# A transformer block in float32: where norm steps, value transfers and loads stand among the attention slots

## The chip, the cores and the metric

The kernel runs on one core of a Trainium2 chip, in float32. The metric is the device time of one execution in microseconds (us), lower is better. The times of the kernel before are the median of three runs.

## What is computed

One transformer block for x of 2 × 1024 × 256 with a context of 2 × 154 × 192 and 16 heads of 64. Cut to what matters:

```python
h = layernorm(x, ln1_g, ln1_b)
x = attention(h, h, sa_wq, sa_wk, sa_wv, sa_wo, sa_bo) + x      # 1024 keys
h = layernorm(x, ln2_g, ln2_b)
x = attention(h, ctx, ca_wq, ca_wk, ca_wv, ca_wo, ca_bo) + x    # 154 keys
h = layernorm(x, ln3_g, ln3_b)
a, gate = split(h @ ff_w1 + ff_b1)
return a * gelu(gate) @ ff_w2 + ff_b2 + x
```

`attention` projects q, k and v, takes a softmax of q k / 8 for every head, weighs v with it, and projects the heads together through `wo`. `layernorm` subtracts the mean of a row of 256, divides by its deviation, and applies a gain and a shift.

## The kernel before

The work runs in *units*: a unit is one batch and one pair of heads, 16 in all (units 0 to 7 are batch 0). The main loop goes through three stages, each in *slots*: 128 slots of self attention (`SA`, eight a unit, two *halves* of `SH` = 4), 48 of context attention (`CA`, three a unit), 64 of the feed-forward part (`FF`). Rows are counted in tiles of 128, eight tiles a batch.

A slot p of self attention does this. TensorE computes the scores of two groups of rows (`scores`, L442) into two PSUM tiles, of which the next slot's scores want the same memory. VectorE takes their maxima (L602), ScalarE the exponents (L453, four instructions), and four small DMAs on SP's queue (`exchange`, L463) carry maxima and sums between partitions. GpSimd and ScalarE join them (`join`, L471 to L479), VectorE takes a reciprocal `rd` (L549), GpSimd scales the weights (L553, four instructions), VectorE transposes them (L567). Two slots later (`LAG` = 2) `self_values` weighs the values with them (L489, `po`); it takes two slots of each four. In the other slots `run_work` gives TensorE a *piece*: for the next unit a query projection (`pq`, L327), a key projection (`pk`, also L327), the values (`pv`, L352), or a tile of the output projection (`py`, L420). These are queues in Python, and the order in which they are emptied is the order of instructions: `work` holds pieces, `outs` output tiles, `side` norm steps, `later` small leftovers (bias additions), `stores`, `adds` and `lates` the second halves of things begun earlier.

`run_work(n, n_side, bank)` takes pieces from `work` worth n banks, then up to `n_side` steps from `side`, whose needs must be met (the output tiles that they read must have been added to x), then output tiles. In self attention it is called in slots 0, 1, 4 and 5 of each unit (and in all of the first half of unit 0), with `n_side` 1.

A normalization is made beside other work, `norm_beside` building its steps. For context attention's batch 0 and for self attention a step concerns one tile, for context attention's batch 1 (not `narrow`) two. A step has up to four parts, for different tiles: `stats` on VectorE (L210, L211), `deviation` (L216, L220), `normalize` (L223: `off` on VectorE at L226, then `xn` on ScalarE at L235, one instruction a tile), and `turn`, four TensorE transposes into a bank (`ph`, L244) whose store (L254, L258) writes `hT`, the input of the projections.

Values of a unit are projected by `project_self_values`, either whole or in two half pieces (`parts` = 2 for the units 1 to 4, that is while `ui < HP`, with `HP` = 4). Its store copies the result on ScalarE (L361) and then sends each copy across to the other half of the partitions by transfers on SP's queue (L365, L366), per tile for a half piece, and for all tiles at once for a whole one.

`self_beside(ui)` runs at the start of each unit and fills the queues: pieces for the next unit, output tiles of a batch and half that are ready, the self norm of batch 1 at `ui == 1` and the context norm of batch 0 at `ui == NPAIR + HP` (12). `load_ahead` issues weight loads for the unit after next. At the seam, `self_drain` finishes the last slots of self attention inside the first slots of context attention. `cross_beside` fills the queues in context attention, loads its keys' and values' weights, and starts the context norm of batch 1.

At the very start x is loaded by both DMA queues, and the columns of the first norm's gain and shift by ACT's queue (L105 to L110).

Of the kernel before, what the change touches and what calls it, by code (L numbers as in the profile page):

```python
# [9 lines left out]
AF = mybir.ActivationFunctionType  # L10
# [8 lines left out]
def tile_transformer_block(ctx: ExitStack, tc: tile.TileContext, a: dict, out: bass.AP):  # L19
# [84 lines left out]
        load_x(nc.scalar, 0, NT // 2 + t)  # L104
    for n in names[:2]:  # L105
        for r0 in range(0, P, HR):
            nc.scalar.dma_start(
                out=cols[r0:r0 + HR, row_of[n]:row_of[n] + NH],
                in_=w[n].rearrange("(r p) -> p r", p=HR),
            )  # L110
# [80 lines left out]
    def norm_pieces(kind, b, first=False):  # L191

        ln = {"sa": "ln1", "ca": "ln2", "ff": "ln3"}[kind]
        g0, b0 = row_of[ln + "_g"], row_of[ln + "_b"]
        st = {}
        nh = NC if kind == "ff" else NH  # L200
        order = tile_order(kind)

        def stats(t):
            if t == 0:
                st["hT"] = hT[kind, b] = p2.tile(
                    [P, nh, NC * S // nh], F32, tag="hT", name=f"hT_{ln}_{b}")
            if t % 2 == 0:
                st["mv", t] = small.tile([P, 2, 2], F32, tag="mv", name=f"mv_{ln}_{b}_{t}")
            s6 = small.tile([P, 6], F32, tag="st", name=f"st_{ln}_{b}_{t}")
            nc.vector.bn_stats(s6, xt[b, order[t] // GT][:, order[t] % GT, :])  # L210
            nc.vector.bn_aggr(st["mv", t // 2 * 2][:, t % 2, :], s6)  # L211

        def deviation(t):
            mv = st["mv", t]
            var = small.tile([P, 2], F32, tag="var", name=f"var_{ln}_{b}_{t}")
            (nc.vector if first else nc.gpsimd).tensor_scalar(  # L216
                var, mv[:, :, 1], EPS, 1.0, op0=ALU.add, op1=ALU.mult
            )
            rstd = small.tile([P, 2], F32, tag="rstd", name=f"rstd_{ln}_{b}_{t}")
            nc.gpsimd.tensor_tensor(rstd, var, power, ALU.pow)  # L220
            st["rstd", t] = rstd

        def normalize(t):  # L223
            rstd = st["rstd", t]
            off = small.tile([P, 2], F32, tag="off", name=f"off_{ln}_{b}_{t}")
            nc.vector.scalar_tensor_tensor(  # L226
                off, st["mv", t][:, :, 0], -1.0, rstd, op0=ALU.mult, op1=ALU.mult
            )
            pool, tag = (one, "xn") if narrow(kind, b) and not first else (pp_, "P")

            xn = pool.tile([P, nh, 2, D // nh], F32, tag=tag, name=f"xn_{ln}_{b}_{t}")
            st["xn", t] = xn
            for i in range(2):
                xs = xt[b, order[t + i] // GT][:, order[t + i] % GT, :]
                nc.scalar.activation(  # L235
                    xn[:, :, i, :], xs.rearrange("p (c d) -> p c d", c=nh), AF.Identity,
                    bias=off[:, i:i + 1], scale=rstd[:, i:i + 1],
                )

        def turn(t):  # L240
            ph = spare["bank"](f"ph_{ln}_{b}_{t}").rearrange("p (c k) -> p c k", c=nh)
            for i in range(2 * D // P):

                nc.tensor.transpose(  # L244
                    ph.rearrange("p c k -> p (c k)")[:, i * P:(i + 1) * P],
                    st["xn", t].rearrange("p c i d -> p (c i d)")[:, i * P:(i + 1) * P], ident)

            def store():
                k = NC * 2 * P // nh
                for c in range(nh):  # L250
                    own = st["hT"][:, c, t // 2 * k:(t // 2 + 1) * k]
                    gain, shift = cols[:, g0 + c:g0 + c + 1], cols[:, b0 + c:b0 + c + 1]
                    if first and (c < nh // 2 or t % 4 == 0):
                        nc.vector.tensor_scalar(  # L254
                            own, ph[:, c, :], gain, shift, op0=ALU.mult, op1=ALU.add
                        )
                    else:
                        nc.scalar.activation(  # L258
                            own, ph[:, c, :], AF.Identity, bias=shift, scale=gain
                        )  # L260

            return store

        return (
            [lambda t=t: stats(t) for t in range(NT)],
            *([lambda t=t, f=f: f(t) for t in range(0, NT, 2)] for f in (deviation, normalize, turn)),
        )

# [6 lines left out]
    def narrow(kind, b):  # L275

        return kind == "sa" or kind == "ca" and b < B - 1
# [68 lines left out]
    def project_self_values(v, pv, wt, h, i0, n):  # L346

        for i in range(i0, i0 + n):
            for c in range(NH):
                for r in range(2):  # L350
                    own = slice(r * HR, (r + 1) * HR)
                    nc.tensor.matmul(  # L352
                        pv[r][:, i * P:(i + 1) * P], lhsT=h[own, c, i * P:(i + 1) * P],
                        rhs=wt[own, c, :], start=(c == 0), stop=(c == NH - 1),
                        tile_position=(r * HR, 0),
                    )

        def store():
            tiles = [slice(r * GT + i0, r * GT + i0 + n) for r in range(2)]
            for r in range(2):  # L360
                nc.scalar.copy(  # L361
                    v[:, tiles[r], 0, :],
                    pv[r][:, i0 * P:(i0 + n) * P].rearrange("p (t d) -> p t d", d=P))
            for own in [slice(0, NT)] if n == GT else tiles:
                nc.sync.dma_start(out=v[:QG, own, 1, :], in_=v[QG:, own, 0, :])  # L365
                nc.sync.dma_start(out=v[QG:, own, 1, :], in_=v[:QG, own, 0, :])  # L366

        return store

# [126 lines left out]

    work, outs = [], []
    side, lates = [], []
    stores, adds = [], []
    later = []  # L500

# [5 lines left out]
    def flush(queue):  # L507
        for fn in queue:
            fn()
        queue.clear()  # L510
# [22 lines left out]
    def out_pieces(kind, b, half, tiles):  # L533
        outs.extend(lambda t=t: out_piece(kind, b, half, t) for t in tiles)
# [79 lines left out]

    def self_beside(ui):

        parts = 2 if ui < HP else 1
        nxt = self_pieces(*units[ui + 1], parts) if ui + 1 < NU else cross_pieces(*units[0], KB)
        if ui + 1 < NU:
            work.extend(nxt)  # L620
        else:

            work.extend(nxt[:1])
            held.extend(nxt[1:])
        if ui >= HP:
            ob, oh = divmod((ui - HP) // HP, 2)
            t0 = (ui % HP) * 2
            out_pieces("sa", ob, oh, (t0, t0 + 1))
        if ui == 1:
            norm_beside("sa", 1)  # L630
        if ui in (HP, HP + 2):
            add_biases("sa", (ui - HP) // 2)
        if ui == NPAIR + HP:
            norm_beside("ca", 0)

    def load_ahead(p):

        ui, n = divmod(p, 2 * SH)
        for what in "qkv":
            at = {"q": 2, "k": 3, "v": 2 * SH - 1}[what] + 3 * (ui == 0 and what != "v")  # L640
            if n != at:
                continue
            if ui + 2 < NU:
                load_weights("sa", units[ui + 2][1], what)
            elif ui + 2 == NU or what == "q":
                load_weights("ca", units[ui + 2 - NU][1], what)

    def self_drain(p):

        late = scale_groups(*joins.pop(0)) if joins else None  # L650
        if p - LAG < SA:
            turn_groups(p - LAG)
        if late:
            late()


    CG = [(t, min(TG, NT - t)) for t in range(0, NT, TG)]
# [168 lines left out]
    def cross_beside(ui):  # L826

        if ui + 1 < NU:
            for what in "kv":
                load_weights("ca", units[ui + 1][1], what)  # L830
            pieces = cross_pieces(*units[ui + 1])
            work.extend(pieces[:2])
            held.extend(pieces[2:])
        if ui == 3:
            norm_beside("ca", B - 1)
        if ui > HP + 1:
            ob, oh = divmod((ui - HP - 2) // HP, 2)
            t0 = ((ui - HP - 2) % HP) * 2
            out_pieces("ca", ob, oh, (t0, t0 + 1))
        if ui == NPAIR + HP + 1:  # L840
            norm_beside("ff", 0)
# [97 lines left out]
    with tc.manual_schedule():  # L939
# [45 lines left out]
        for p in range(SA):  # L985
# [15 lines left out]
            load_ahead(p)  # L1001
            h, hg = divmod(p, SH)
            if h == 0 or hg < LAG:
                run_work(2 if p < SA - SH else 1, 1, sum_tile)
            else:
                run(lambda: self_values(h - 1, hg - LAG))

        for c in range(CA):
# [21 lines left out]
            flush(adds)  # L1030
            then = cross_first(c)
            flush(stores)
            flush(lates)
            lates.append(then())
            if c <= SH:
# [69 lines left out]
```

## Time and profile before

| What | us |
|---|---|
| median of three runs | 1174.38 (1170.46 to 1174.64) |
| the profiled execution: its own time | 1176.44 |
| the profiled execution: its span, from first to last instruction | 1174.6 |

The stages of that execution, by windows that begin at the first instruction of a slot:

| Stage | from to | length | PE busy |
|---|---|---|---|
| start, up to the first scores | 0.00 to 20.35 | 20.35 | 14.84 |
| self attention, slots 0 to 7 | 20.35 to 64.46 | 44.11 | 39.95 |
| slots 8 to 16 (first slot of unit 2) | 64.46 to 115.52 | 51.06 | 44.17 |
| units 12 to 14 | 553.94 to 690.72 | 136.78 | 134.84 |
| unit 15 | 690.72 to 732.90 | 42.18 | 39.78 |
| context attention, first five slots | 732.90 to 755.31 | 22.41 | 19.96 |
| context attention, the rest | 755.31 to 975.56 | 220.25 | 213.72 |
| feed-forward | 975.56 to 1174.60 | 199.04 | 195.49 |

The page names engines by short names: PE is TensorE's matrix multiplication, PEld its weight load, DVE VectorE, ACT ScalarE, POOL GpSimd, SP the engine that here only issues DMAs. A name with q, such as SPq, is an engine's queue of issues. "L442" is a line of the kernel. A number in brackets after a line is idle time of the engine before it, and the arrow says what ended it.

### The profile page before, as it was taken

What the parts mean: (1) busy time and instruction counts of PE and PEld (TensorE: products, weight loads), DVE (VectorE), ACT (ScalarE), POOL (GpSimd) and SP (SyncE); (2) the same over time, 40 slices, a digit from 0 to 9 for tenths busy, and PEclk for the clock granted to TensorE, in tenths of its full rate; (3) what the DMA queues carried; (4) which work ended last, traced back from release to release, by engine and by line L of the source; (5) the groups of instructions that cost most, each with busy time, mean ns of one, the idle gap of its engine ahead of it and who ended that gap; (6) DMA issues with size and microseconds to landing.
All of it is one profiled execution on the core that took longest, in us unless ns stands there. A gap on an engine that the chain in (4) does not pass through costs nothing.

```text
span 1174.6 us, 36750 instructions
## 1 busy us (share of the span) xinstructions
PE 1135.7 (97%) x14343; PEld 684.0 (58%) x14343; DVE 834.8 (71%) x1184; ACT 653.0 (56%) x2095; POOL 666.4 (57%) x1556
## 2 busy tenths in 40 slices
PE   8889999999999999999999999998999999999998
PEld 5444444455555545545545554564666667888887
DVE  4778988889898998989998899556565674232222
ACT  5656777666665665756666766547655573041111
POOL 1657777787887777777777777546454453030000
PEclk9989999999999999999999999999999999999999
DMA  2231111111111111101101010157544443000000
GB/s 77 74 92 30 39 30 30 37 33 39 30 35 39 30 31 39 39 21 39 46 14 39 25 28 16 46 138 183 139 116 112 112 93 73 1 18 10 18 9 18
DMA packets 105215, 59.94 MB, mean 51 GB/s; under 512 B 32394, under 2 KB 95826, under 8 KB 105042
## 3 DMA queue, kind: packets, MB, share of 16 engines
q1 hardware_dynamic: 101138, 54.84, 19.6%
q10 hardware_dynamic: 3904, 2.76, 0.8%
q8 instruction: 113, 1.85, 0.7%
q14 instruction: 60, 0.49, 0.1%
HBM read 27.91 MB, written 2.10 MB: 26 GB/s over the span
## 4 chain that ended last, share of the span: by engine, by line
PE 72%; ACT 9%; DMA 5%; POOL 4%; DVE 3%; SPq 3%; issue 3%; ACTq 0%; DVEq 0%; POOLq 0%
PE po L489 14%; PE s L442 12%; PE pa L894 9%; ACT p L453 6%; PE py_ca L420 5%; PE pq_ca L327 5%; PE pf L917 5%; PE py_sa L420 4%; DMA st<-st 4%; PE poc L807 4%; PE pv_sa L352 3%; PE sc L728 3%; PE pq_sa L327 3%; SPq L463 2%; PE pk_sa L327 2%
## 5 line engine op out<-in xcount | busy, mean ns | idle before, releaser
L453 ACT ACTIVATE p<-s,st 128x512 f32<-128x512 f32 x512 | 344.9, 687 | 201.8 <-DVE st L602 198.7
L553 POOL TENSOR_SCALAR p<-p,rd,ee 128x512 f32<-128x512 f32 x512 | 385.6, 767 | 44.7 <-DVE rd L549 43.7
L602 DVE TENSOR_REDUCE st<-s 128x2 f32<-128x1024 f32 x256 | 301.4, 1219 | 32.3 <-PE s L442 17.2
L567 DVE STREAM_TRANSPOSE pT<-p 128x1024 f32<-128x1024 f32 x256 | 302.4, 1219 | 1.5 <-POOL p L553 1.5
L442 PE MATMUL s<-k_sa,q_sa 64*32 64x512 f32 x4096 | 257.1, 597 | 19.3 <-ACT p L453 18.2
L489 PE MATMUL po<-pT,v_sa 64*64 64x256 f32 x4096 | 235.8, 379 | 0.0
L489 PEld LDWEIGHTS po<-pT,v_sa 64*64 64x64 f32 x4096 | 150.4, 133 | 109.1 <-issue 34.4
L755 POOL TENSOR_SCALAR p<-p,rden 128x154 f32<-128x154 f32 x256 | 96.8, 398 | 117.0 <-DVE rden L752 116.5
L442 PEld LDWEIGHTS s<-k_sa,q_sa 64*32 64x32 f32 x4096 | 63.8, 106 | 145.8 <-ACT p L453 68.7
L744 ACT ACTIVATE p<-sc,neg 128x154 f32<-128x154 f32 x256 | 95.7, 394 | 83.2 <-DVE rden L752 77.5
L894 PE MATMUL pa<-hT_ln,wf 128*128 128x256 f32 x512 | 121.0, 379 | 0.0
L903 DVE SCALAR_TENSOR_TENSOR u<-pa,cols,gate 128x256 f32<-128x256 f32 x64 | 31.0, 484 | 124.4 <-ACT gate L900 124.4
L900 ACT ACTIVATE gate<-pa,cols 128x256 f32<-128x256 f32 x64 | 30.3, 473 | 151.5 <-PE pa L894 151.5
L894 PEld LDWEIGHTS pa<-hT_ln,wf 128*128 128x128 f32 x512 | 96.8, 190 | 13.7 <-DVE u L903 0.4
L453 ACT ACTIVATION_READ_ACCUMULATOR p<-s,st 128x1 f32 x512 | 104.6, 204 | 0.0
L733 DVE TENSOR_REDUCE neg<-sc 128x6 f32<-128x924 f32 (+1 forms) x48 | 48.6, 1012 | 56.0 <-PE sc L728 55.9
L352 PEld LDWEIGHTS pv_sa<-sa_wv,hT_ln 64*128 64x128 f32 x1024 | 59.6, 188 | 19.9 <-issue 8.4
L327 PE MATMUL pq_ca<-hT_ln,ca_wq 64*128 64x512 f32 (+1 forms) x304 | 64.9, 616 | 5.1 <-ACT hT_ln L258 3.0
L477 POOL TENSOR_TENSOR zz<-ee,st 128x8 f32<-128x8 f32 x128 | 25.9, 202 | 73.6 <-ACT ee L475 73.6
L352 PE MATMUL pv_sa<-sa_wv,hT_ln 64*128 64x128 f32 x1024 | 64.0, 276 | 1.8 <-ACT k_sa L341 1.2
L917 PE MATMUL pf<-wf,u 128*128 128x256 f32 x256 | 65.0, 379 | 0.2 <-DVE u L903 0.2
L549 DVE RECIPROCAL rd<-den 128x4 f32<-128x4 f32 x128 | 22.6, 177 | 57.2 <-POOL den L479 51.7
(80 smaller groups left out, 1289.1 us busy)
## 6 DMA issues: line engine op xcount, KB each, us to landing
wf<-pT_ca SPq DMA_DIRECT2D x128, 128.0 KB, 2.5
st<-st SPq DMA_DIRECT2D x512, 1.0 KB, 1.8
v_sa<-v_sa SPq DMA_DIRECT2D x22, 256.0 KB, 3.5
sa_wq<-in_L_xattn_sa_wq_dram SPq DMA_DIRECT2D x32, 128.0 KB, 3.0
sa_wk<-in_L_xattn_sa_wk_dram SPq DMA_DIRECT2D x32, 128.0 KB, 3.3
sa_wv<-in_L_xattn_sa_wv_dram SPq DMA_DIRECT2D x32, 128.0 KB, 3.5
ca_wq<-in_L_xattn_ca_wq_dram SPq DMA_DIRECT2D x32, 128.0 KB, 2.9
wf<-in_L_xattn_ff_w_dram SPq DMA_DIRECT2D x12, 256.0 KB, 3.5
```

What stands on the lines that cost most here:

```text
L327: nc.tensor.matmul(pq[r][f:f + m, t0:t0 + n], lhsT=wt[own, c, f:f + m], rhs=h[own, c, t0:t0 + n], start=(c == 0), stop=(c == NH - 1), tile ...
L352: nc.tensor.matmul(pv[r][:, i * P:(i + 1) * P], lhsT=h[own, c, i * P:(i + 1) * P], rhs=wt[own, c, :], start=(c == 0), stop=(c == NH - 1), ...
L420: nc.tensor.matmul(py[:, :D], lhsT=o[:, i, t * P:(t + 1) * P], rhs=wo[kind][:, half * HP + i, :], start=(i == 0), stop=(i == HP - 1),)
L442: nc.tensor.matmul(sc[a4 * KB:(a4 + 1) * KB, j, :], lhsT=q[r, c:c + KB], rhs=k[r, h * HB:(h + 1) * HB], start=True, stop=True, tile_positi ...
L453: nc.scalar.activation(pr[:, j, :], sc[:, j, :], AF.Exp, bias=st[:, 0, 0, i, j:j + 1], accum_out=st[:, 0, 1, i, j:j + 1],)
L489: nc.tensor.matmul(po[a2][j * DH:(j + 1) * DH, :QH // 2], lhsT=v[r, t, e, j * DH:(j + 1) * DH], rhs=pT[r, j * NK + n, :], start=(t == 0 an ...
L553: nc.gpsimd.tensor_scalar(pr[:, j, :], pr[:, j, :], rd[:, c:c + 1], ee[:, 0, c:c + 1], op0=ALU.mult, op1=ALU.mult,)
L567: nc.vector.transpose(halves[h][:, :, c:c + KB], groups.pop(0).rearrange("p j (n k) -> p (j n) k", k=KB))
L602: nc.vector.tensor_reduce(st[:, 0, 0, i, :], sc[i], AX.X, ALU.max, negate=True)
L755: nc.gpsimd.tensor_scalar(pr_[:, j, i, :T], pr_[:, j, i, :T], rden[:, j, i:i + 1], 1.0, op0=ALU.mult, op1=ALU.mult,)
L894: nc.tensor.matmul(pa[:, half, :TF * P], lhsT=w1[:, c, half * DF + f * P:half * DF + (f + 1) * P], rhs=h[:, c, t0 * P:(t0 + TF) * P], star ...
L917: nc.tensor.matmul(sums[blk][i][:, :D], lhsT=sums[blk, "u"][:, f, i * P:(i + 1) * P], rhs=w2[:, f, :], start=(f == 0), stop=(f == NF - 1),)
```

## The change

- The columns of `ln1_b` are loaded by SP's queue instead of ACT's.
- The two transfers of values across partitions come once a unit, after the last copy, for all tiles.
- `parts` is 2 only for `0 < ui < HP`: unit 1's values, made in unit 0, come in one piece. The first unit then has six pieces.
- `run_work` is called with `n_side` of 1 only in slots 4 and 5 of a unit (`h` odd) and in the first half of unit 0; in slots 0 and 1 it takes no norm step.
- The context norm of batch 0 begins at unit 9 instead of unit 12. Output tiles are made in the order 0, 4, 1, 5, …, the one in which the norm reads them.
- In the context norm of batch 1, `xn` is made on GpSimd by a multiply and an add with per-row scalars, instead of on ScalarE.
- The key weights of context attention's unit 1 are loaded in slot 126, instead of in the first slot of context attention.
- At the seam, the reciprocal and the scaling of `self_drain` are put behind the first reduction of the next slot.

```diff
-            nc.scalar.dma_start(
+            (nc.scalar if n == names[0] else nc.sync).dma_start(
...
-                nc.scalar.activation(
-                    xn[:, :, i, :], xs.rearrange("p (c d) -> p c d", c=nh), AF.Identity,
-                    bias=off[:, i:i + 1], scale=rstd[:, i:i + 1],
-                )
+                xs, own = xs.rearrange("p (c d) -> p c d", c=nh), xn[:, :, i, :]
+                if kind == "ca" and not narrow(kind, b):
+                    nc.gpsimd.tensor_scalar(
+                        own, xs, rstd[:, i:i + 1], off[:, i:i + 1], op0=ALU.mult, op1=ALU.add)
+                else:
+                    nc.scalar.activation(
+                        own, xs, AF.Identity, bias=off[:, i:i + 1], scale=rstd[:, i:i + 1])
...
-            for own in [slice(0, NT)] if n == GT else tiles:
-                nc.sync.dma_start(out=v[:QG, own, 1, :], in_=v[QG:, own, 0, :])
-                nc.sync.dma_start(out=v[QG:, own, 1, :], in_=v[:QG, own, 0, :])
+            if i0 + n == GT:
+                nc.sync.dma_start(out=v[:QG, :, 1, :], in_=v[QG:, :, 0, :])
+                nc.sync.dma_start(out=v[QG:, :, 1, :], in_=v[:QG, :, 0, :])
...
+    drain = []
...
-        parts = 2 if ui < HP else 1
+        parts = 2 if 0 < ui < HP else 1
...
-            out_pieces("sa", ob, oh, (t0, t0 + 1))
+            out_pieces("sa", ob, oh, tile_order("ca")[t0:t0 + 2])
...
-        if ui == NPAIR + HP:
+        if ui == NPAIR + 1:
             norm_beside("ca", 0)
...
+        if p == SA - 2:
+            load_weights("ca", units[1][1], "k")
...
-        late = scale_groups(*joins.pop(0)) if joins else None
+        if joins:
+            drain.append(scale_groups(*joins.pop(0)))
         if p - LAG < SA:
             turn_groups(p - LAG)
-        if late:
-            late()
...
-            for what in "kv":
+            for what in "kv" if ui else "":
...
-                run_work(2 if p < SA - SH else 1, 1, sum_tile)
+
+                run_work(2 if p < SA - SH else 1, h % 2 or h == 0, sum_tile)
...
             flush(stores)
+            flush(drain)
             flush(lates)
```

## The prediction

> **What bounds the kernel now.** I read the page first, then busy time by stage, then the timeline and the waits of the stages in which TensorE is not full.
>
> From the page of the kernel before:
>
> ```profile
> span 1174.6 us, 36750 instructions
> ...
> PE 1135.7 (97%) x14343; PEld 684.0 (58%) x14343; DVE 834.8 (71%) x1184; ACT 653.0 (56%) x2095; POOL 666.4 (57%) x1556
> ...
> PE 72%; ACT 9%; DMA 5%; POOL 4%; DVE 3%; SPq 3%; issue 3%; ACTq 0%; DVEq 0%; POOLq 0%
> ```
>
> TensorE is the bound, and 38.9 us of the span are not covered by it. The chain that ended last still leaves TensorE for 28% of its length, so single places run on other engines. The windows (start and end; length, PE busy and matmuls; granted clock; DMA share; GB/s), cut at slot starts, tell where:
>
> ```profile
> 64.46:115.52 51.06, 44.17 (x709) 0.93 0.22 54
> 115.52:160.96 45.44, 42.70 (x716) 1.00 0.14 33
> ...
> 293.14:336.58 43.44, 43.44 (x724) 1.00 0.15 34
> ...
> 553.94:597.75 43.81, 43.68 (x725) 1.00 0.14 33
> 597.75:644.93 47.18, 45.85 (x733) 1.00 0.14 31
> 644.93:690.72 45.79, 45.31 (x733) 1.00 0.13 29
> ...
> 732.90:755.31 22.41, 19.96 (x164) 0.92 0.17 48
> ...
> 799.57:815.34 15.77, 13.47 (x109) 0.89 0.60 140
> 815.34:833.60 18.26, 15.53 (x117) 0.91 0.60 154
> ```
>
> A unit of self attention (eight slots) costs 43.44 us where nothing waits. The first full one, at 64.46, costs 51.06; units 13 and 14 (597.75 and 644.93) carry eight more matmuls, the norm's turns, and cost 3.4 and 2.0 us more than unit 12; then come the seam between the attentions (732.90) and the context attention around its norm (799.57 to 833.60). The clock is below 1.00 in just the windows with long waits. The feed-forward part, 199.04 us with 195.49 busy, is untouched.
>
> Why slots 7 to 9 are slow, from the timeline (start, length, engine, operation; in brackets the idle time and what ended it):
>
> ```profile
> 61.20 0.60 SPq L365 DMA_DIRECT2D v_sa<-v_sa  x1
> 61.85 0.60 SPq L366 DMA_DIRECT2D v_sa<-v_sa  x1
> 62.61 3.39 SPq L463 DMA_DIRECT2D st<-st  x4
> ...
> 67.31 0.20 POOL L471 TENSOR_TENSOR dd<-st 128x4 f32<-128x4 f32 x1 [3.48 <-DMA st<-st]
> ...
> 68.04 0.21 ACT L475 ACTIVATE ee<-dd 128x8 f32<-128x8 f32 x1 [3.15 <-POOL dd L473]
> ...
> 71.90 0.66 PE L442 MATMUL s<-k_sa,q_sa 64*32 64x512 f32 x8 [3.51 <-ACT p L453]
> ```
>
> Value transfers occupy SP's queue, the exchange of maxima (`st`) goes out behind them, GpSimd waits for it, then ScalarE, then the scores.
>
> And in context attention, two lines of its timeline:
>
> ```profile
> 801.20 1.09 ACT L235 ACTIVATE xn_ln<-x,off_ln,rstd_ln 128x256 f32<-128x256 f32 x2 [1.80 <-DVE off_ln L226]
> ...
> 803.37 1.20 PE L327 MATMUL pq_ca<-hT_ln,ca_wq 64*128 64x512 f32 x2 [1.89 <-ACT v_ca L701]
> ```
>
> ScalarE stands still before `xn`, and the copies of `v_ca` behind it hold a bank that TensorE's query projection wants. The waits of that stretch also name `hT_ln` (2.7 us), made on ScalarE after `xn`.
>
> **What the Trainium skill says.** "TensorE: Matmul & The Clock Gate", section "HAM oscillation — how this bites in real kernels": idle gaps of over about 3.4 us throttle TensorE. The trace agrees in kind: from 76 to 82 us it shows a clock of 0.68, from 804 to 809 of 0.72, from 820 to 825 of 0.66, each behind such waits. So a long wait costs its length plus (1 − 0.68) × 6.0 = 1.9, 1.4 and 1.7 us. "DMA: Bandwidth & Descriptors", "Issuing engines are not separate DMA queues": issuing elsewhere saves sequencer time only. Here an issue takes 0.60 us on SP, so fewer issues help although the bytes stay. "GPSIMD Engine Reference", 3.1: 512 elements of a one-input operation took 769 ns; the trace has 767 ns (L553). "SBUF — State Buffer", "SBUF: two separate sides": a GpSimd operation and some VectorE ones exclude each other; no wait in this trace shows it for `xn`, and it is my upper cost there.
>
> **Part by part.** The order of instructions of the two kernels shows equal numbers of matmuls and VectorE operations; SP issues about 27 transfers fewer. So everything comes from waits. Sums are against the profiled execution, 1176.44 us (span 1174.6), 2.06 above the median of 1174.38.
>
> 1. *Column loads of ln1_b go from ACT's to SP's queue.* ACT issued them from 4.74 to 6.01 and loaded its table at 6.04; the first `xn` ran at 7.34, its `off` ready at 6.74. Gain at most 7.34 − 6.74 = 0.6; on SP they delay sa_wq, so 0 is the other end. −0.4.
>
> 2. *Two value transfers a unit, six pieces in the first unit.* Four of 64 KB (4 × 0.62 = 2.5 us of SP) stood behind each half. Now two of 256 KB (1.06 + 0.64 us, as at 278.91) follow the second half: 3.3 us of SP less in each halved unit. Unit 1's values, which before had their second half in slot 8, come whole in slot 5, and all later pieces move one slot up. Slot 8 (64.46 to 71.90) lasts 7.45 us with 3.75 of TensorE work (scores and a half piece), slot 9 (to 81.16) 9.26 with 5.17: 3.7 + 4.1 of stall, slow clock included, and I take these 7.8 as gone. Of the rest in units 1 to 4 (idle 6.89 + 2.74 + 1.25 + 1.49 = 12.37, plus 1.9 of clock, less 7.8 = 6.5) I take a fifth, 1.35: half pieces remain in units 1 to 3, now in neighbouring slots (4 and 5), and there TensorE has only 3.75 us of work in a slot whose loop takes 5.28 (rd to reduce 0.27, 1.26 to exp, 2.66 to ee, 0.30, 0.28, 0.28, 0.23). Against this, outputs start at slot 37 instead of 45, and 3.65 us of `py_sa` work (two tiles of 8 matmuls, 1.83 each) comes in from the seam. −7.8 − 1.35 + 3.65 = −5.5, range −2 to −9. Late next: the landing of `st` beside weight loads (that at 67.61 landed after 4.70 us, against a median of 1.8).
>
> 3. *Norm steps only in slots 4 and 5 of a unit.* Batch 1's self norm moves from slots 8 to 28 to slots 12 to 52, so units 5 and 6 receive steps: a turn and some loop time, +0.5 (0 to +2). The context norm of batch 0 starts at unit 9, not 12, in slots 76 to 116, in pairs every eight slots where it had pairs every four. A step adds to the slot's loop statistics (0.58 on DVE), `off` (0.2), `xn` on ACT (1.09) and hT (4 × 0.38 = 1.5 over ACT). Slots 4 and 5 carry values and outputs, 5.65 and 5.53 us of TensorE, against 5.17 and 5.15 for q and k; and scores can start about 2.0 us after the exponents that free their bank. Units 13 and 14 exceeded unit 12 by 5.35; 1.3 I leave for turns and remains. −4.0, range 0 to −5. hT is complete at slot 116 in both, needed at 120.
>
> 4. *Seam.* ca_wk is loaded at slot 126: the wait for it was 2.45 us. The two `py_sa` tiles have left (3.65; paid above). `rd` and scale go behind the first reduction of the next slot, which frees the exponents (5.7 us of waits there) but delays the last transposes by about one reduction of 1.0 us. The clock of 0.92 over 22.41 us costs 1.8. Possible 2.45 + 3.65 + 1.8 = 7.9; I take −5.5, range −3 to −7.
>
> 5. *`xn` of context attention on GpSimd.* Eight operations 128x256. No row has this form; between 398 ns (128x154) and 767 ns (128x512) a line gives 398 + 102/358 × 369 = 503. Lower bound 398, upper 767. So 4.0 us on an engine that idles 115 us there for `rden`; p's scaling queued behind it may be late by a pair, 1.0. ScalarE loses 8 × 0.597 and the wait of 1.80. Gone at most: idle 2.30 + 2.73 + 0.45, clock 1.4 + 1.7 = 8.6. hT stays on ScalarE, so I take −6.5, range −2.5 to −8.6; with `xn` waiting for the shared ports, near −2.5.
>
> Sum: −0.4 − 5.5 + 0.5 − 4.0 − 5.5 − 6.5 = −21.4: 1155.0 for the profiled execution, **1153** from the median.
>
> **Rivals.** *A, the next wait takes over*: the exchange's landing or the 5.28 us loop holds slots 8 to 35, and hT the context slots. For it: half pieces stay, and 4.70 us of landing had weights beside it, not values alone. Then parts 2 and 5 give −2 and −2.5, the rest −0.4 + 0.5 − 4.0 − 3.5: −11.9, about 1163. *B, more goes*: all of part 2's waits (−9), the seam at −7, the context stage at −8.6, and units 9 to 14 at −5: −30, about 1144. Against it: every wait found so far had another close behind. *C, slower*: two adjacent norm steps use up the slack of 2.0 us in all 11 pairs or singles from slot 12 to 116, each delaying the exchange once more. It takes more than 3.1 us a group to outweigh the other gains (17.9 of parts 1, 2, 4 and 5, plus the 15.8 by which the slots with norm steps of before exceed their TensorE work, over 11); at 3.6 a group, 11 × 3.6 − 15.8 = +24 against −18, 1180. For it: ScalarE's 3.6 of exponents, 1.1, 1.5 and a value copy of 1.06 fill 7.2 us of a 5.6 us slot. Against: it was so in pairs of before, which cost 5.35 in two units. *D, no effect*: late loads or the clock keep the stalls, 1172.
>
> **Numbers.** Chances: forecast (1148 to 1158) 0.52, A (1158 to 1168) 0.24, B (1140 to 1148) 0.14, D 0.06, C 0.04. The range 1143 to 1166 holds the forecast, most of A and over half of B. Half a per cent, 1168.5 to 1180.3, is about what a measurement of this kernel can tell from no change. Faster: 0.52 + 0.24 + 0.14 + a part of D, 0.91; same 0.05, slower 0.04.
>
> **What would show it.** Unit windows of 43 to 45 us from slot 9 on, without `ACT p` waits over 2 us, confirm part 2; clocks of 1.00 in slots 10 and 142; units 13 and 14 near 44 confirm part 3; no wait for `ca_wk` part 4; `xn` at about 0.5 us on POOL and no `pq_ca` wait for `v_ca` part 5. I am wrong if pairs of slots 12 and 13 exceed 13 us, if `st` still lands late at slots 7 to 9, or if `hT_ln` waits grow.

## The result, and the profile after

The changed kernel took 1155.78 us (median of four runs, 1154.65 to 1160.22) against 1173.95 for the kernel before (four runs): a ratio of 0.9858 with a 95% interval of 0.9824 to 0.9892. Run again later beside others it took 1158.94 against 1174.69, a ratio of 0.9858 (0.9837 to 0.9879). It is faster by 1.4%, 16.7 us by the ratio. The forecast was 1153, with 1148 to 1158 as its range: the first median lies in it, the second just above.

The page of the changed kernel, the lines that answer to those shown of before:

```profile
span 1152.6 us, 36693 instructions
...
PE 1124.7 (98%) x14343; PEld 683.3 (59%) x14343; DVE 833.9 (72%) x1184; ACT 650.3 (56%) x2085; POOL 670.5 (58%) x1564
...
PE 83%; ACT 5%; POOL 4%; DVE 2%; issue 2%; DMA 2%; SPq 1%; DVEq 0%; ACTq 0%; POOLq 0%
```

TensorE does as many matmuls as before (x14343), and its share of the chain that ended last rose from 72% to 83%: what went is waiting on others. Its busy time fell by 11.0 us with the same matmuls, in part because fewer of them ran at a lowered clock (17.1 us of the trace of before are at half clock, none of that of after between 8 us and its last 1.2); the ends of matmuls are modelled in the profile, so busy time is not a measure of work alone.

The windows of the changed kernel, cut at the same work as those of before (start and end; length, PE busy and matmuls; clock; DMA share; GB/s):

```profile
63.98:110.45 46.47, 41.84 (x708) 1.00 0.24 59
110.45:154.25 43.80, 40.92 (x708) 1.00 0.15 33
...
333.04:376.48 43.44, 43.44 (x724) 1.00 0.16 37
594.88:638.91 44.03, 44.03 (x728) 1.00 0.15 33
638.91:682.96 44.05, 44.05 (x728) 1.00 0.13 30
...
725.14:742.26 17.12, 14.83 (x149) 1.00 0.23 64
786.51:798.76 12.25, 11.17 (x110) 1.00 0.77 180
798.76:812.26 13.50, 13.50 (x118) 1.00 0.81 205
```

Unit 1 went from 51.06 to 46.47 us, units 13 and 14 from 47.18 and 45.79 to 44.03 and 44.05, the first five context slots from 22.41 to 17.12, the slots of the context norm from 15.77 and 18.26 to 12.25 and 13.50. The clock is 1.00 in all of these windows. A unit with no stall still costs 43.44.

For a ledger I take the starts of VectorE's maximum reductions, one kind in self attention and one in context attention, which the timelines of both kernels show in equal number:

| Stretch | before | after | difference | predicted |
|---|---|---|---|---|
| to the first reduction | 21.55 | 21.41 | −0.14 | −0.4 |
| slots 0 to 40 (units 0 to 4) | 229.41 | 224.65 | −4.76 | −5.5 |
| slots 40 to 56 (units 5, 6) | 87.03 | 88.23 | +1.20 | +0.5 |
| slots 56 to 104 (units 7 to 12) | 261.02 | 261.84 | +0.82 | |
| slots 104 to 120 (units 13, 14) | 92.96 | 88.09 | −4.87 | −4.0 for units 9 to 14 |
| context slots 0 to 4 (the seam) | 22.42 | 17.11 | −5.31 | −5.5 |
| context slots 12 to 19 (the norm) | 39.68 | 30.86 | −8.82 | −6.5 |

The stretches left out are equal to 0.01 us, but for the end behind the last context reduction, which is 0.17 shorter. The sum is −21.9, so the two profiled executions agree with the forecast of −21.4 almost term by term. The medians differ by less, because this execution of the changed kernel was one of its best. That, and whether the terms have the causes that were given for them, is what the runs below are about.

### The profile page after: what moved, and what is told of

It reads as the page before. It is cut to its first block, busy times and chain, and to the rows that moved or that the text cites. A ratio compares the mean times of both kernels' runs of the same rounds, so it can differ in the third digit from the quotient of the medians.

```text
span 1152.6 us, 36693 instructions
## 1 busy us (share of the span) xinstructions
PE 1124.7 (98%) x14343; PEld 683.3 (59%) x14343; DVE 833.9 (72%) x1184; ACT 650.3 (56%) x2085; POOL 670.5 (58%) x1564
## 4 chain that ended last, share of the span: by engine, by line
PE 83%; ACT 5%; POOL 4%; DVE 2%; issue 2%; DMA 2%; SPq 1%; DVEq 0%; ACTq 0%; POOLq 0%
PE po L492 16%; PE s L445 16%; PE pa L899 10%; PE py_ca L423 5%; PE py_sa L423 5%; PE pf L922 5%; PE pq_ca L330 5%; PE pk_sa L330 4%; PE poc L812 4%; PE pv_sa L355 4%; PE pq_sa L330 4%; ACT p L456 4%; PE sc L733 3%; DMA st<-st 2%; DVE st L606 2%
## 5 line engine op out<-in xcount | busy, mean ns | idle before, releaser
L445 PE MATMUL s<-k_sa,q_sa 64*32 64x512 f32 x4096 | 254.4, 595 | 13.2 <-ACT p L456 12.2
L423 PE MATMUL py_ca<-ca_wo,o_ca 128*128 128x256 f32 x256 | 60.8, 384 | 0.3 <-ACT hT_ln L261 0.3
L330 PE MATMUL pq_ca<-hT_ln,ca_wq 64*128 64x512 f32 (+1 forms) x304 | 60.5, 591 | 0.2 <-ACT hT_ln L261 0.2
```

What stands on the lines that cost most here:

```text
L330: nc.tensor.matmul(pq[r][f:f + m, t0:t0 + n], lhsT=wt[own, c, f:f + m], rhs=h[own, c, t0:t0 + n], start=(c == 0), stop=(c == NH - 1), tile ...
L423: nc.tensor.matmul(py[:, :D], lhsT=o[:, i, t * P:(t + 1) * P], rhs=wo[kind][:, half * HP + i, :], start=(i == 0), stop=(i == HP - 1),)
L445: nc.tensor.matmul(sc[a4 * KB:(a4 + 1) * KB, j, :], lhsT=q[r, c:c + KB], rhs=k[r, h * HB:(h + 1) * HB], start=True, stop=True, tile_positi ...
```

## Experiments

### How much of a stretch is chance

> The changed kernel once more, for a time beside the other three and a second trace of the same program. Expected 1155 to 1160. Where its first trace had 8.27 us for slot 9 and 17.1 us from the first to the fifth reduction of context attention, a second trace shows how much of single stages is spread: theory (both hang on when transfers land) 1 to 3 us apart in these two places, none elsewhere; rival (fixed) under 0.3.

Measured: 1158.94 us (1154.53 to 1160.69). In the second trace slots 0 to 40 take 226.94 us (first: 224.65) and the seam 18.76 (17.11); the stretch of the context norm takes 30.87 (30.86), slots 104 to 120 88.52 (88.09). So the two places differ by 2.3 and 1.7 us, as expected. At the seam this second trace has these windows (behind the number of matmuls in brackets stands the clock):

```profile
733.23:736.64 3.41, 1.79 (x16) 1.00 0.54 157
736.64:740.05 3.41, 3.41 (x18) 0.50 0.03 11
```

The clock of TensorE fell to half for 3.41 us, and so it did in two more places: from 36.91 us, in slot 3, and from 74.45, behind the stall of slot 9. The landing of transfers was only half of my explanation. Nor is the clock all of it: the run below with the keys' load moved back has no fall in its trace, and still 226.72 us for slots 0 to 40. A third trace with the same instructions there (the run below with `xn` on ScalarE) shows what it costs at the seam:

```profile
737.74 1.91 PE L733 MATMUL sc<-k_ca,q_ca 64*128 64x154 f32 x12 [1.38 <-ACT k_ca L684]
739.44 5.78 PE L330 MATMUL pq_ca<-hT_ln,ca_wq 64*128 64x512 f32 x16
```

and the timeline of the changed kernel's first trace at the same place:

```profile
734.22 1.06 PE L733 MATMUL sc<-k_ca,q_ca 64*128 64x154 f32 x12 [1.37 <-ACT k_ca L684]
735.11 3.60 PE L330 MATMUL pq_ca<-hT_ln,ca_wq 64*128 64x512 f32 x16
```

The waits are equal, 1.37 and 1.38 us; the scores and the query projection behind them take 7.7 us in one (1.91 + 5.78), where the clock was at half for 6.83 us, and 4.7 in the other. The Trainium skill, "TensorE: Matmul & The Clock Gate", section "What's actually happening", says that the window over which activity is judged is free-running. Then it would be chance where a gap falls in it, and the traces agree: in the first one the periods of 3.41 us, counted from where its clock rose at 7.99 us, cut the same waits elsewhere, and leave TensorE busier (2.04 us of a period, against 1.79 ahead of the fall in the second trace):

```profile
731.62:735.03 3.41, 2.04 (x24) 1.00 0.55 164
735.03:738.44 3.41, 3.41 (x20) 1.00 0.01 4
```

The last section has all traces. The page's rule of idle gaps over about 3.4 us does not describe them: here two waits of 0.92 and 1.37 us were enough in some executions.

Over seven traces whose instructions are those of the changed kernel up to slot 40 (both of its own, and `xn` on ScalarE, `xn` twice, keys' load, drain and idle transposes below), slots 0 to 40 take 224.65 to 228.66, median 227.05. Against the one trace of before (229.41) the typical gain there is thus 2.4 us, not 4.8. Over seven traces with the same seam (both, `xn` on ScalarE, `xn` twice, norm slots, transfers, and the divided load) the seam takes 17.11 to 20.14, median 18.66: 3.8 gained, not 5.3. The clock sorts them: 17.11 without a fall, 18.55 to 18.82 in the five with 3.41 us of half clock, 20.14 in the one with 6.83.

### The context norm on GpSimd

```diff
-                if kind == "ca" and not narrow(kind, b):
+                if False:
```

> The changed kernel with xn of the second context norm on ScalarE again, all else as changed. Theory (ScalarE's wait for off, with the value copies and hT queued behind xn, held TensorE): same times up to the tenth context slot, then two slots long again (about 8.2 and 9.1 us) and a clock under 1.00 behind them; 7 to 9 us more than the changed kernel, about 1164. Rival (the earlier seam and loads, not the engine of xn, shortened that stage): under 3 us more, at most 1158.5.

Measured: 1167.72 us (1166.50 to 1168.69), ratio to before 0.9924 (0.9910 to 0.9939). The stretch of the norm is 38.01 us instead of 30.86: 7.15 lost, the rival is out. By the ratios the total is 7.8 us longer, inside the 7 to 9 expected. Some 1.7 of the 7.15 are the price of one fall of the clock, to half for 3.41 us from 812.10, with TensorE busy throughout. Its waits of TensorE in the stretch:

```profile
PE pq_ca L330 <- ACT hT_ln L261: 3.0, 2, 2.7
PE pq_ca L330 <- ACT v_ca L706: 2.1, 2, 1.9
```

Both are ScalarE's, in the columns microseconds, times and longest. In the changed kernel the same view has 0.2 us for `hT_ln`, though its copies are still on ScalarE, and nothing for `v_ca`. The timeline of the changed kernel there:

```profile
787.40 3.68 PE L330 MATMUL pq_ca<-hT_ln,ca_wq 64*128 64x512 f32 x15
...
789.12 1.08 POOL L237 TENSOR_SCALAR xn_ln<-x,rstd_ln,off_ln 128x256 f32<-128x256 f32 x2
```

The projection starts at 787.40, before `xn` does: ScalarE's value copies (from 786.62 there) no longer stand behind `xn`. The row of `xn` on GpSimd has 548 ns each.

Is GpSimd's time free? The same operation twice:

```diff
-                    nc.gpsimd.tensor_scalar(
-                        own, xs, rstd[:, i:i + 1], off[:, i:i + 1], op0=ALU.mult, op1=ALU.add)
+                    for _ in range(2):
+                        nc.gpsimd.tensor_scalar(
+                            own, xs, rstd[:, i:i + 1], off[:, i:i + 1], op0=ALU.mult, op1=ALU.add)
```

> The changed kernel with every xn of the second context norm made twice on GpSimd, the second time over the first: 8 more operations, 4.3 us by the trace's 0.54 each. Theory (GpSimd has room in that stage, and what was gained is the queue on ScalarE): from the thirteenth to the twentieth reduction of context attention at most 1 us longer than the 30.86 of the changed kernel. Rival (the turns wait for xn, and the scaling of p stands behind it, so GpSimd's time counts at once): 3 to 5 us longer.

Measured: 1162.50 us (1161.46 to 1164.49), ratio 0.9898 (0.9860 to 0.9936). The stretch takes 33.50 us, 2.64 more for 4.3 us of work: between the two theories, and nearer to the rival. But its trace has a fall of the clock in this stretch, for 3.41 us from 804.96 with TensorE busy throughout, which costs some 1.7 of the 2.64; without it the stretch would be 0.9 longer, as the theory had it. Ahead of the fall stands this wait of TensorE:

```profile
PE ph_ln L248 <- POOL xn_ln L238: 2.6, 1, 2.6
```

In the changed kernel the same wait is already 1.1 us, with no fall behind it. By the ratios the total is 4.7 us longer, with intervals that overlap. GpSimd's long idle time in this stage is not at the moment when the turn wants `xn`.

### Transfers or pieces in the first units

```diff
-            if i0 + n == GT:
-                nc.sync.dma_start(out=v[:QG, :, 1, :], in_=v[QG:, :, 0, :])
-                nc.sync.dma_start(out=v[QG:, :, 1, :], in_=v[:QG, :, 0, :])
+            for own in [slice(0, NT)] if n == GT else tiles:
+                nc.sync.dma_start(out=v[:QG, own, 1, :], in_=v[QG:, own, 0, :])
+                nc.sync.dma_start(out=v[QG:, own, 1, :], in_=v[:QG, own, 0, :])
```

> The changed kernel with the value transfers per tile and per half again (8 a half piece instead of 2 after the second), the six pieces of the first unit kept. Theory (the transfers' issues hold the exchange of maxima on SP's queue): each of the three units with halves longer by 2 us or more, SP queue lines of v_sa ahead of st, GpSimd waits for st of 2 us and more there; 4 to 8 us more, about 1162. Rival (the place of the pieces decides, the transfers hide): under 1.5 us more, at most 1157.3.

Measured: 1158.55 us (1157.09 to 1158.80), ratio 0.9844 (0.9830 to 0.9859), no slower than the changed kernel's 0.9858. Slots 0 to 40 take 225.78, inside the spread of the changed kernel. My theory fell: where the halves stand in slots 4 and 5 of a unit, the smaller transfers (of 64 KB, 32 by the trace, so four a half piece; the expectation had eight) cost nothing that shows. Unit 1's values stay whole in this kernel, so it says nothing of the first unit.

From the other side, on the kernel before: both edits, and the pieces alone.

```diff
-        parts = 2 if ui < HP else 1
+        parts = 2 if 0 < ui < HP else 1
```

> The kernel before with only the two value transfers a unit and the six pieces in the first unit. Theory (these two alone bring the early part): first score of slot 40 earlier by 4 to 6.5 us though two more output tiles' work is done by then, and 3 to 4 us at the seam from those tiles; 7 to 10 less than before, about 1165. Rival (the norm steps in slots 8, 9, 16, 17 held these units): slot 40 earlier by under 2.5 us, total at least 1168.

> The kernel before with only the six pieces in the first unit; its transfers per tile and per half stay. Theory after the runs so far (the place of the pieces decides, the transfers count for 1 us at most): within 1.5 us of the kernel before with both, so 6 to 9 less than before. Rival (the transfers on SP's queue are what held slots 7 to 10): slot 8 to 10 as slow as before, total less than 5 us below before and that from the two output tiles at the seam.

Measured: with both 1168.61 us (1167.78 to 1171.00), ratio 0.9937 (0.9920 to 0.9953); with the pieces alone 1169.56 (1167.95 to 1171.28), ratio 0.9953 (0.9937 to 0.9968). Slots 0 to 40 take 226.37 and 226.54 us, 3.0 and 2.9 less than before, where I had expected 4 to 6.5. The edit of the pieces alone brings the early part; the edit of the transfers adds 0.2 us in the traces and nothing that the intervals separate. But the first of them is not free of the second: unit 1's values, now whole, also cross by two transfers of 256 KB instead of eight of 64. No run takes these two apart.

What the runs do show is that a stall in slots 8 and 9 stays without the small transfers. From the scores of slot 8 to those of slot 10, in the kernel before, in that with both edits and in the changed one:

```profile
64.46:81.16 16.70, 12.49 (x165) 0.80 0.43 112
...
65.52:80.30 14.78, 11.18 (x196) 1.00 0.38 107
...
63.98:77.95 13.97, 11.03 (x190) 1.00 0.42 114
```

TensorE is idle there for 4.21 us before, and still for 3.60 and 2.94; with the pieces alone for 2.61.

The seam takes 20.75 and 20.02 us instead of 22.42, less short than the 3.65 us of output tiles that left it. With both edits the clock was at half there for 6.83 us, against 3.41 before; with the pieces alone for 3.41, but TensorE's waits there are 3.57 us instead of 2.45.

### What still holds slot 9

The chain of the changed kernel between 57 and 80 us (start, length, what) and its timeline:

```profile
66.58 6.22 DMA st<-st
```

```profile
65.82 0.37 ACTq L120 DMA_DIRECT2D sa_wo<-in_L_xattn_sa_wo_dram  x1
...
73.02 0.20 POOL L474 TENSOR_TENSOR dd<-st 128x4 f32<-128x4 f32 x1 [3.11 <-DMA st<-st]
...
74.49 3.72 PE L330 MATMUL pk_sa<-hT_ln,sa_wk 64*32 64x512 f32 x57 [2.38 <-ACT q_sa L340]
```

The exchange of slot 7 landed after 6.22 us. No value transfer is near it; the 1 MB of `sa_wo` is, and two loads of 128 KB of `sa_wv` (from 67.28), which the next kernel keeps. So the load of `sa_wo` was cut in four and moved:

```diff
-        later.append(lambda: load_out("sa", nc.scalar))
...
+            if p in (16, 17, 24, 25):
+                load_out_part((16, 17, 24, 25).index(p))
```

> The changed kernel with the 1 MB load of sa_wo cut into four of 256 KB, issued in slots 16, 17, 24 and 25 instead of one in slot 8. Theory (the exchange of slot 7 lands 5.9 us after its issue because that load runs beside it): GpSimd's wait for st of 3.1 us in slot 9 goes, slot 9 takes 5.2 to 6 us instead of 8.27, nothing new in slots 16 to 25; 2 to 3 us less. Rival (weights of the next unit, or the loop of 5.28 us itself, hold slot 9): under 0.8 less.

Measured: 1156.59 us (1154.22 to 1156.87), ratio 0.9837 (0.9823 to 0.9852). The same step in its timeline, without a wait:

```profile
71.30 0.20 POOL L481 TENSOR_TENSOR dd<-st 128x4 f32<-128x4 f32 x1
```

From the reduction of slot 8 to that of slot 10 it takes 10.08 us. The twelve traces in which the load is whole, that of the kernel before among them, show 11.86 to 16.04. Between the scores of the two slots TensorE is idle for 0.64 us, against 2.38 to 4.21 in those twelve:

```profile
65.33:76.75 11.42, 10.78 (x196) 1.00 0.18 48
```

Slots 24 to 36, where parts land beside the halves, take 67.11 us, 0.9 more than in the changed kernel's first trace; but its other traces and those with the same instructions there reach 67.44, so no loss is shown. The median is 2.4 below that of the changed kernel run beside it, as expected, but the intervals overlap. The step from the reduction of slot 7 to that of slot 8 is still 7.25 us long (6.43 to 8.30 in all fourteen traces); what holds it was not tried.

### The norm's slots

```diff
-                run_work(2 if p < SA - SH else 1, h % 2 or h == 0, sum_tile)
+                run_work(2 if p < SA - SH else 1, 1, sum_tile)
...
-        if ui == NPAIR + 1:
+        if ui == NPAIR + HP:
```

> The changed kernel with a norm step allowed in slots 0 and 1 of a unit again, and the first context norm starting at unit 12 again. Theory (norm steps beside the short query and key slots exhaust the slack): units 13 and 14 longer by 4 to 5 us together, units 5 and 6 shorter by 1.5 to 2, units 1 to 3 longer by 0 to 3; sum 2 to 6 more, 1158 to 1161. Rival (output tiles in the norm's order, or the pieces standing one slot earlier, made units 13 and 14 short): those units stay at 44.0 us, the sum is 2 less to 1 more.

Measured: 1158.56 us (1156.59 to 1159.12), ratio 0.9844 (0.9829 to 0.9859). The totals cannot tell it from the changed kernel; the stretches can. Windows of units 13 and 14 in this kernel:

```profile
593.99:640.14 46.15, 45.09 (x733) 1.00 0.14 32
640.14:685.25 45.11, 45.01 (x732) 1.00 0.13 29
```

Against 44.03 and 44.05, 3.2 us are back, less than the 4 to 5 expected, of the 4.9 by which these units fell. Slots 40 to 56 are 0.5 shorter and 56 to 104 also 0.5: what this part of the change brings is some 2 us. In slots 0 to 40 the kernel took 225.43, so norm steps in slots 8 and 9 did no harm there. What the remaining 1.7 of units 13 and 14 are was not tried. This kernel took 90.96 for slots 104 to 120, and the kernels before with both edits and with the pieces only, which have the old norm slots too, 91.27 and 91.62, against 92.96 before. All three have the six pieces, so the place of the pieces may be the rest of it, or the spread of the one trace of before.

### The seam

```diff
-        if p == SA - 2:
-            load_weights("ca", units[1][1], "k")
...
-            for what in "kv" if ui else "":
+            for what in "kv":
```

> The changed kernel with the second unit's context key weights loaded in the first slot of context attention again. Theory (the load stands behind the value transfers on SP's queue and lands too late): a wait of TensorE for ca_wk of 2 to 3 us in the second or third context slot, 2 to 4 us more than the changed kernel. Rival (the wait only uncovers another, for the exponents or keys there): under 0.8 more.

Measured: 1156.18 us (1155.45 to 1156.95), ratio 0.9840 (0.9827 to 0.9854), no slower than the changed kernel beside it. Its timeline:

```profile
734.22 0.76 PE L678 MATMUL pk_ca<-ctxT,ca_wk 96*128 96x154 f32 x4 [2.46 <-DMA ca_wk<-in_L_xattn_ca_wk_dram]
```

The wait for the load is back with 2.46 us (before: 2.45), and the seam takes 17.15 us, as in the changed kernel's first trace with 17.11. There, in its place, stood waits of 0.92 for `q_ca` and 1.37 for `k_ca`, 2.29 together: the theory had the wait right and its price wrong, and the rival holds.

```diff
-            flush(drain)
...
-        if joins:
-            drain.append(scale_groups(*joins.pop(0)))
+        late = scale_groups(*joins.pop(0)) if joins else None
         if p - LAG < SA:
             turn_groups(p - LAG)
+        if late:
+            late()
```

> The changed kernel with reciprocal and scaling of the last self-attention slots ahead of the next context reduction again. Theory (the reduction that frees the exponents waits behind the reciprocal): second and third context reduction 1 to 2 us later, 1 to 2.5 us more in all. Rival (TensorE has other work there): under 0.5.

Measured: 1161.20 us (1154.91 to 1162.35), ratio 0.9874 (0.9852 to 0.9897). The second context reduction is 0.7 us later than in the changed kernel, the third comes 1.1 sooner after it, so by the third the order of before is ahead by 0.4. Behind it, TensorE's waits for `q_ca` and `k_ca` are 0.65 and 2.33 us, 2.98 together against 2.29. The clock is at half for 3.41 us, and the seam takes 19.50, 0.7 to 1.0 more than in the five traces that have the change's order and as long a fall: less than the 1 to 2.5 expected, and from one trace. Four of its five runs are above 1160 and one took 1154.91. Whether the old order makes a fall more likely is not settled: that fastest run had a mean clock of 0.995, the others 0.996 and 0.997.

### Keeping the clock

```diff
+            if c == 3:
+                busy(9, again)
             then = cross_first(c)
...
+            if c == 1:
+                again = sum_tile("again")
+                busy(6, again)
             run_work(2, 1, n_sum=2 * (SH < c < 2 * NPAIR and c % len(CG) == 0))
```

> The changed kernel with 15 idle TensorE transposes of the identity, 6 and 9, put into the two waits at the seam (before the second unit's keys and before its first scores). They compute nothing that is used. Theory (some executions lose the TensorE clock in these gaps and then run the query projection in 5.1 to 5.8 us instead of 3.6): the projection always takes 3.6, the fastest execution stays at 1154.5, the median falls by 1 to 3 us and the spread shrinks. Rival (the waits themselves cost, the clock is a by-product, or the added work delays the scores): median not lower, fastest execution 0.5 to 2 us higher.

Measured: 1157.68 us (1156.56 to 1158.55), ratio 0.9854 (0.9838 to 0.9869). Its windows:

```profile
76.00:82.00 6.00, 6.00 (x65) 0.53 0.02 3
733.00:740.00 7.00, 6.68 (x61) 1.00 0.34 95
```

The seam kept its clock and took 17.08 us, with 2.07 us of matmuls that serve nothing. The total did not fall: this trace lost the clock in slot 3 and for 6.83 us in slot 9, with 0.53 in the window above and 228.66 us for slots 0 to 40. The expectation for the total failed, and the rival's held, with a fastest execution of 1156.56; that for the place held in the one trace.

Both remedies together, with the parts of `sa_wo` in slots 32, 33, 48 and 49:

> As the last, and sa_wo in four parts of 256 KB in slots 32, 33, 48 and 49, where no half pieces stand any more, instead of one of 1 MB in slot 8. Theory: slot 9 near 5.3 us as in the kernel with the parts in slots 16 to 25, without that one's later losses in slots 24 to 36; median 2 to 4 us below the changed kernel, 1152 to 1155. Rival (the time saved in slot 9 is lost again in the half slots behind it): median within 1 us of the kernel with the idle transposes alone.

Measured: 1154.51 us (1154.41 to 1155.72), ratio 0.9830 (0.9814 to 0.9845). Slots 8 to 10 again take 10.08, slots 0 to 40 224.79, the seam 17.36; its projection:

```profile
735.40 3.60 PE L337 MATMUL pq_ca<-hT_ln,ca_wq 64*128 64x512 f32 x16
```

Its four runs lie within 1.3 us, at the fast end of the changed kernel's eight (1154.53 to 1160.69). By the ratios it is 0.28% or 3.3 us below the changed kernel; the intervals still overlap, so a gain of the median is likely and not proved. Nor do the runs tell it from the kernel with the divided load alone (0.9837, 0.9823 to 0.9852): what the transposes add to the total is not shown.

## Why the prediction was right, point by point

*Bound and sum.* The matmuls stayed and the waits went, as argued; 1155.78 against 1153; the second median, 1158.94, lies in rival A's range. That the terms fit the first trace so well is luck, since its clock never fell: typical executions gain 2.4 us where I put 5.5, and 3.8 where I put 5.5, and the norm's 8.8 where I put 6.5 makes up for half of that.

*Part 1* was right in size: the first reduction comes at 20.81 to 21.41 us in the eleven traces with the load on SP's queue, and at 21.55 to 22.00 in the three with it on ACT's.

*Part 2* failed in the step that took the 7.8 us of slots 8 and 9 as gone with the issues of value transfers. With both edits, and no small transfer left, TensorE still stood idle there for 3.60 us, and for 2.94 in the changed kernel. The edit of the pieces brings what is gained, and going back to small transfers in the later halves costs nothing; what unit 1's own transfers had cost is not shown. What held slot 9 in the changed kernel is what the prediction named as "late next", as a part of rival A and as a sign of being wrong: `st` landing late beside weight loads. The run with `sa_wo` divided shows it.

*Part 3* was right in place and near in size: units 13 and 14 gave 4.9, units 5 and 6 took 1.2, and units 7 to 12, where I put nothing, 0.8. By the run with the old slots some 2 us of the net belong to the norm's slots.

*Part 4*: the sum was right in the first trace, and two of its terms not. The 2.45 us for `ca_wk` are worth 0, since `q_ca` and `k_ca` come no sooner. What remains fits: 3.65 for the two output tiles, and 22.42 − 3.65 − 17.11 = 1.66 for the clock, where the trace of before has one fall under full work, 3.41 us at half clock or 1.7 lost. The reciprocal's new place is worth 0.7 to 1.0 by the one trace with the old order, so the terms do not add up without rest. And the clock part is gained only in some executions.

*Part 5*: mechanism right, and size short. I left 2.1 us for `hT` on ScalarE; its wait fell from 2.7 to 0.2 us with `xn` gone from ahead of it. Of the 8.82, 7.15 came back with `xn` on ScalarE; the kernels before with both edits and with the pieces alone took 37.97 and 39.71 for the stretch, so 1.7 of it is spread, and the clock explains it: 3.41 us at half clock in this stretch in the traces with about 38, twice that in those with 39.7. The change also took away what brings these falls: wherever a period of 3.41 us is laid in the stretch, TensorE is busy for 0.68 of it or more in the changed kernel's first trace, and for as little as 0.20 with `xn` on ScalarE. The duration, 503 estimated, was 548 ns. For 4.0 us on an idle engine I allowed 1.0 of delay; of an added 4.3, 2.64 counted, some 1.7 of them through the clock.

*The clock.* The prediction put its three falls behind gaps of over about 3.4 us. TensorE's waits ahead of them were 3.51, 1.89 and 2.73 us, so only the first is that long, and the trace did not agree with the rule. The price was near for the last two, 3.41 us at half clock with TensorE busy throughout, or 1.7 us each, against 1.4 and 1.7; the first fall lasted 6.83 us and cost some 3.1 (half of 2.71 + 3.41 busy), not 1.9.

*Rivals.* C found nothing in its favour: the pair of slots with norm steps in unit 13 took 11.8 us (6.24 and 5.53), with TensorE busy throughout. B describes the first trace in the context stage only.

## What to carry to other kernels

A wait that ends last is worth what the next waits behind it leave: put it back alone before crediting it, as 2.45 us of load wait proved to be worth nothing. An exchange of 1 KB on the critical loop should not meet a load of 1 MB: here it landed after 6.22 us, against a median of 1.8. Divide the load, and issue it elsewhere; which of the two helped was not tried apart. Where TensorE has short waits in a row, the same program takes several times, by how often the clock falls, so compare stretches of traces and clocks before comparing medians a few microseconds apart.

## What the hardware showed that was not expected

The granted clock has two values in these traces, 1.00 and 0.50, and falls in whole periods. In the fourteen traces it falls 26 times (the start and the end not counted), each time for 3.41 or 6.83 us, and in each trace the starts lie whole multiples of 3.413 us apart. Ahead of every fall TensorE was busy for at most 0.54 of such a period, by the modelled ends; every period under 0.47 outside a fall was followed by one, and between these shares both happen. So what counts here is the share of a period, and not the length of one wait.

That orders what looked like chance. At the seam, two waits of 0.6 to 1.0 and 1.4 to 1.6 us brought a fall in six of seven traces, for a price of 1.4 to 3.0 us. The single wait of 2.46 us brought none in its one trace, where two periods shared it (TensorE busy for 2.00 and 2.36 us of 3.41); the same wait of 2.45 in the trace of before did. Fifteen useless transposes (2.07 us) held the clock in both traces that had them: wherever a period is laid in that stretch, TensorE is busy for 0.91 and 0.82 of it or more, against 0.44 at the least in the changed kernel's first trace. The stretch was as long as with full clock and without them (17.08 and 17.36 against 17.11).
